# A graph layer woven into an MLP: the account that deals out its steps begins lower at a raised rate, with two more empty steps before the first weights

## The chip, the cores and the metric

One core of a Trainium2 chip runs the whole program in one launch. The metric is device microseconds (us) of one execution. TensorE (PE) does the matmuls, and its weight loads (PEld) overlap them. VectorE (DVE), ScalarE (ACT) and GpSimd (POOL) do the rest, and each engine works through its own queue in order. DMAs are issued from the queues of SP, ACT and POOL. TensorE's clock can be throttled, and the profile gives the clock that was granted as a share of full speed.

## The reference

The input is `x` with 1250 tokens of 768 features, and a graph of 21250 edges (`src`, `dst`, self loops among them, to which the graph layer adds another set). All is float32. With `xn = layernorm(x)`:

```python
# two graph attention layers; n = 1250
e = leaky_relu(s_src[src] + s_dst[dst], 0.2)
emax = segment_max(e, dst); ee = exp(e - emax[dst])
alpha = ee / segment_sum(ee, dst)[dst]
out = segment_sum(alpha * h[src], dst) + bias       # 4 heads of 192, then 2 heads of 96
gnn = concat([xn, out2]) @ Wu + bu
...
# linear attention with 12 heads, then an MLP 768 -> 3072 -> 768 with gelu
h = xn + linear_attention(layernorm(xn))
mix = h + gelu(layernorm(h) @ fc1_w + fc1_b) @ fc2_w + fc2_b
...
x = x + gnn + mix
x = x + two_of_four_experts(layernorm(x))           # 768 -> 1536 -> 768, routed by the pooled tokens
```

## The kernel before

Tokens lie in 10 tiles of 125. Both graph layers are computed densely: a table in DRAM holds for each pair (source, target) how many edges there are. It is made by 170 indirect DMAs from POOL's queue (L311), alternately into two tables, which are later added into one (`merged`, L1224), 125 rows at a time. POOL issues these merges behind the last of the indirect DMAs.

The stages, in order: features, keys, values and queries, the attention's output, the MLP of the mix, and the experts. The graph layers have no stage of their own. They are written as a generator, `gnn()`, and their steps are dealt out between the matmuls of the MLP of the mix:

- **The MLP.** 12 groups of 256 hidden units (`GROUPS`), each in two parts of the tokens (`MIX`, 2 x 250 and 2 x 375 columns). `fc1_unit` makes seven products of three matmuls each (a matmul in float32 is two instructions in the profile), with sums by Strassen's scheme, in the letters `P` of a pattern. Its evacuations are copies on ACT (L1152, L1162, L1165), sums on DVE (L1155, L1168, L1175) and Gelus on ACT (L1135). `fc2_half` (letter `h`) multiplies hidden units with half the columns of `fc2_w` for one tile of tokens (L1186, four instructions) and adds the sum to the result on DVE (L1191). Its PSUM tile is one of three banks, which `bank()` also hands to the transposes of the graph's steps. `load_fc1` (L898, 768 KB) and `load_fc2` (L905) load weights from SP's queue. DVE makes the sums of weights (L115 to L118).
- **The account.** `spend(us)` is called after each product (charged 2.04 or 1.36 us) and each half (1.39 us). It adds `rate * us` to a credit. While the credit covers the price of the last step, it pays it and takes the next step from `gnn()`, which yields its own price. So the account sets where in the program's text a graph step stands. A scheduler then orders the instructions of each engine; what is wrapped in `pin` keeps its order.
- **A search (`largest`)**, once for each graph layer: the largest source score for each target. It issues the first merges (first search only) and fetches of the table (`fetch`, L1237, POOL), yields a `lead` (17 us in the first search), and then goes through 10 pieces of 125 sources: one DVE instruction that masks the piece (L1252), and one for each head that takes the maximum (L1260 for the first piece, L1256 for the others), 10 us charged for a piece with four heads, 4.5 with two. Then come transposes (L1270) and reductions (L1274), a few small sums, a transpose of the result to one row (L1290), a copy (L1294), and the row's write to DRAM (`b_d`, L1295, from ACT's queue).
- **Weights and sums (`weighted`, `lagging`)**: for each head and each of three groups of target tiles, `bt` is read back from `b_d`, broadcast over the partitions (L1303, POOL). For each piece of sources: two exponentials on ACT (L1314, L1317), a maximum and a product with the table on DVE (L1319, L1320), and the matmuls that add up the weighted features (L1364 in the first layer, L1403 in the second), one piece behind the weights. A step is charged 1.7 us. The second layer ends with a projection (L1416) added to the result (L1423).

ACT needs another table for the exponentials than for the Gelus, so a switch between them is an `ACT_TABLE_LOAD`.

When the last group's second part begins, a loop takes all steps that are left at once. After that the tiles' LayerNorm and transposes (`last_tile`) run between the last halves.

Of the kernel before, what the change touches and what calls it, by code (L numbers as in the profile page):

```python
# [32 lines left out]
def tile_gps_layer(ctx, tc, a, out):  # L33
# [52 lines left out]
    def bank(name):  # L86
        return p_mm[0].tile([128, 512], F32, name=name, tag="mm")
# [556 lines left out]
    with tc.tile_pool(name="kvp", bufs=1) as kvp:  # L644
# [185 lines left out]
        for t in range(5):  # L830
            def before(t=t):
                if t == 1:
                    by_tokens(vec, xt, TP, TP)
                if t == 2:
                    by_tokens(vec, xt, 2 * TP, 3 * TP)
                    for vv in vvs:
                        pin(nc.vector.memset(vv[:, :, 128:129], 1.0))
# [379 lines left out]
    def rest(n):  # L1217
        for _ in range(n):
            yield 2.5
# [8 lines left out]
    def largest(heads, s, b_d, pace, before=lambda c: None, behind=lambda: None, lead=9.0):  # L1228


        run = slot_x[:TP, : heads * N].rearrange("p (h n) -> p h n", n=N)
        load = [slot_x[:TP, 5000 + i * N : 5000 + (i + 1) * N] for i in range(2)]
        load.append(turns[:TP, 0, :N])

        def fetch(c):
            if c < NT:
                pin(nc.gpsimd.dma_start(load[c % 3], adj_d[c * TP : (c + 1) * TP, :]))  # L1237

        for c in range(3):
            before(c)  # L1240
        fetch(0)
        fetch(1)
        yield lead
        for c in range(NT):
            before(c + 3)
            fetch(c + 2)
            if c == NT - 1:
                behind()
            adj = load[c % 3]

            far = turns[:TP, 1, :N]
            pin(nc.vector.tensor_scalar(far, adj, -2.0 * NEG, NEG, op0=ALU.mult, op1=ALU.add))  # L1252
            for h in range(heads):
                sc = s[:, 0, h, c : c + 1]
                if c:
                    pin(nc.vector.scalar_tensor_tensor(  # L1256
                        run[:, h, :], far, sc, run[:, h, :], op0=ALU.min, op1=ALU.max
                    ))
                else:
                    pin(nc.vector.tensor_scalar(run[:, h, :], far, sc, None, op0=ALU.min))  # L1260
                if h % 2:
                    yield pace
        yield from rest(2)
        mx = gp.tile([TP, heads, NT], F32, name=f"mx{heads}")
        for h in range(heads):
            for u0 in range(0, NT, 4):
                n = min(4, NT - u0)
                ps = bank("ps_mx").rearrange("p (u c) -> p u c", c=128)
                for u in range(n):
                    pin(nc.tensor.transpose(  # L1270
                        ps[:TP, u, :TP], run[:, h, (u0 + u) * TP : (u0 + u + 1) * TP],
                        ident[:TP, :TP],
                    ))
                nc.vector.tensor_reduce(  # L1274
                    mx[:, h, u0 : u0 + n], ps[:TP, :n, :TP], AX.X, ALU.max
                )
            yield 2.0
        sd = s[:, 1]
        b = gp.tile([TP, 2, heads, NT], F32, name=f"b{heads}")
        m = small.tile([TP, heads, NT], F32, name=f"m{heads}", bufs=1)  # L1280
        nc.vector.tensor_tensor(mx, mx, sd, ALU.add)
        nc.vector.scalar_tensor_tensor(m, mx, 0.2, mx, op0=ALU.mult, op1=ALU.max)
        nc.vector.tensor_tensor(b[:, 0], sd, m, ALU.subtract)
        nc.vector.scalar_tensor_tensor(
            b[:, 1], sd, 0.2, m, op0=ALU.mult, op1=ALU.subtract
        )
        yield from rest(2)
        n = 2 * heads * NT
        ps = bank("ps_row")
        pin(nc.tensor.transpose(  # L1290
            ps[:n, :TP], b.rearrange("p j h t -> p (j h t)"), ident[:TP, :TP]
        ))
        row = small.tile([80, TP], F32, name="row", bufs=1)
        nc.vector.tensor_copy(row[:n], ps[:n, :TP])  # L1294
        nc.scalar.dma_start(b_d, row[:n])  # L1295
        yield from rest(4)

    def weighted(g, h, heads, b_d, s, sl):

# [47 lines left out]
    def gnn():  # L1347
        feats = {}

        def fetch(h):  # L1350
            gh = turns[:TP, h % 2, :].rearrange("p (t f) -> p t f", f=193)
            pin(nc.gpsimd.dma_start(gh, rows(g1_d[h % 4], TP)))
            feats[h % 4] = gh

        yield from largest(4, s1, b1_d, 5.0, merged, lambda: fetch(0), 17.0)
        fetch(1)
        for g, (t0, n) in enumerate(SPLITS):
            for h in range(4):
# [15 lines left out]
                for i in range(n):  # L1374
# [9 lines left out]
                    if h == 3:  # L1384
                        for j in range(2):
# [5 lines left out]
                            nc.vector.tensor_reduce(s2[:, j, :, t0 + i], pr, AX.X, ALU.add)  # L1391
        nc.vector.tensor_scalar(s2l, s2[:, 0], 0.2, None, op0=ALU.mult)
        yield from largest(2, s2, b2_d, 4.5)
        load_wu2x()
        parts = earlier()
# [74 lines left out]


    steps = gnn()
    credit, cost = -44.0, 0.0

    def spend(us):
        nonlocal credit, cost
        credit += 1.06 * us
        while cost is not None and credit >= cost:
            credit -= cost
            cost = next(steps, None)  # L1480
# [15 lines left out]
    def put_half(g, c, t, j):  # L1496
        fc2_half(g, c, t, j)
        spend(1.39)
        if g == GROUPS - 1 and j:
            last_tile(t)  # L1500

    todo = []
    for g in range(GROUPS):
        if g:
            load_fc1(g + 1)
            load_fc2(g, 1)
            load_fc2(g + 1, 0)
        for c, pattern in enumerate(("PPhhhhPhhPPhhPPhhhh", "PPhhPhhPPhhPPhh")):
            if g == GROUPS - 1 and c:
                for _ in steps:  # L1510
                    pass
                cost = None
                gnn_pool.__exit__(None, None, None)
            parts = fc1_unit(g, c)
            if g == 0 and c:
                pattern = "PhPhhPhhhPhhPPP"
            for p in pattern:
                if p == "P":
                    next(parts)
                    if g or c:  # L1520
                        spend(2.04 if c else 1.36)
                elif todo:
                    put_half(*todo.pop(0))
            todo = halves_of(g, c)
# [197 lines left out]
    def second(i, t):  # L1722

        g = slots[i // 3]["g"][:TP]
        w11, w12, s3, w22, s1, s2, s4 = seconds[i]
        h11, t3, h21, h22 = quarters(i)

        def put(o, v):
            pin(nc.vector.scalar_tensor_tensor(o, v, g, o, op0=ALU.mult, op1=ALU.add))  # L1729

        ts = slice(t * TP, (t + 1) * TP)
        t1, t2, t4 = (ht[:, k, :, ts] for k in range(3))
        y1, y2 = y[:, t, :], y[:, t + NT // 2, :]
        p1, p5, p7 = (bank(n)[:TP, :384] for n in ("ps_r1", "ps_r5", "ps_r7"))
        p6 = bank4("ps_r6").rearrange("p a b -> p (a b)")[:TP, :384]
        c1 = u3 = mp.tile([128, 384], F32, name="c1")[:TP]
        u2 = mp.tile([TP, 384], F32, name="v2", bufs=2)
        product(mat, p1, h11[:, :, ts], w11)
        pin(nc.scalar.copy(c1, p1))
        product(mat, p6, t2, s2)  # L1740
        pin(nc.vector.tensor_tensor(u2, p6, c1, ALU.add))
        product(mat, p7, t3[:, :, ts], s3)
        pin(nc.vector.tensor_tensor(u3, p7, u2, ALU.add))
        product(mat, p5, t1, s1)
        put(y2[:, 384:], p5)
        put(y2[:, 384:], u3)
        yield
        product(mat, p1, h21[:, :, ts], w12, more=True)
        put(y1[:, :384], p1)
        product(mat, p7, t4, w22, more=True)  # L1750
        put(y1[:, 384:], p7)
        put(y1[:, 384:], u2)
        product(mat, p5, h22[:, :, ts], s4, more=True)
        put(y2[:, :384], p5)
        put(y2[:, :384], u2)
        yield
# [112 lines left out]
    rest, held, acts = [], [], []  # L1869
    for i in range(6):  # L1870
        for u in range(4):
# [31 lines left out]
            if i and u == 0:  # L1903
                if i > 1:
                    second_sums(i - 1)
                rest = [second(i - 1, t) for t in range(NT // 2)]
# [66 lines left out]
```

## Time and profile before

| | us |
|---|---|
| median of 3 runs (1900.64 to 1905.47) | 1905.28 |
| the profiled execution, its own time | 1904.38 |
| its span, first to last instruction | 1902.6 |
| PE busy, of the span | 1860.4 (98%) |
| DVE busy | 1326.4 (70%) |
| ACT busy | 811.1 (43%) |
| POOL busy | 502.7 (26%) |

An execution is divided into 40 slices of 47.6 us in the page's second part, with a digit for the busy tenths. A busy PE is not PE at its peak, since matmuls are pipelined and a matmul that waits in the pipeline counts as busy. A wait is listed with the engine and the line that ended it; where that one had long been done, it was another, often a DMA.

The last indirect DMA of the table is issued at 571.15, the first three merges at 575.44. The merges are issued on POOL in the order 0, 1, 2, then fetch 0, fetch 1, merge 3, fetch 2, and so on:

```
575.44  merges 0, 1, 2      586.70  fetch 0      593.76  fetch 1
594.29  merge 3             599.73  fetch 2      606.67  fetch 3
```

### The profile page before, as it was taken

The page shows a single profiled execution, that of the slowest core. Times are in us where ns is not written, and L with a number is a line of the kernel's source. Part 1 is how long each engine was busy: PE and PEld are TensorE (multiplying, and loading weights), DVE is VectorE, ACT ScalarE, POOL GpSimd, SP SyncE. Part 2 cuts the span into 40 slices and gives each one's busy share as a digit, 9 for nine tenths or more (in the row PEclk, how much of TensorE's full clock was granted, in tenths as well). Part 3 has the DMA queues.
Part 4 walks back from the last instruction along what each step waited for, and adds up shares of the span by engine and source line. Part 5 has one row for each costly group of instructions (what it writes and reads, how often), then busy time and mean ns, then how long its engine had stood idle before and what let it go on. Part 6 is the DMA issues. An engine that isn't in the chain of part 4 may idle for free.

```text
span 1902.6 us, 19523 instructions
## 1 busy us (share of the span) xinstructions
PE 1860.4 (98%) x6936; PEld 1235.7 (65%) x6936; DVE 1326.4 (70%) x2407; ACT 811.1 (43%) x1231; POOL 502.7 (26%) x341
## 2 busy tenths in 40 slices
PE   8999999999996999999999999999999999999998
PEld 7555556855564667787777655566766666666664
DVE  4656692668534976676766968766777777777778
ACT  3233321333410118777774176655373353433330
POOL 2275666786883120111210111100131000000000
PEclk9999999999998999999999999999999999999999
DMA  9748532526129842232443632201485202011023
GB/s 337 225 94 217 126 86 53 126 16 109 6 26 154 168 122 68 78 101 79 110 105 80 158 90 82 76 13 60 130 98 84 73 0 67 2 66 46 13 87 109
DMA packets 185934, 177.85 MB, mean 93 GB/s; under 512 B 110131, under 2 KB 155243, under 8 KB 184556
## 3 DMA queue, kind: packets, MB, share of 16 engines
q0 software_dynamic: 126640, 68.01, 20.9%
q1 hardware_dynamic: 55918, 100.83, 17.0%
q10 hardware_dynamic: 3278, 7.75, 1.3%
q8 instruction: 55, 0.90, 0.2%
q14 instruction: 43, 0.35, 0.1%
HBM read 140.11 MB, written 42.08 MB: 96 GB/s over the span
## 4 chain that ended last, share of the span: by engine, by line
PE 79%; DMA 7%; POOL 5%; issue 5%; DVE 2%; ACT 1%; ACTq 1%; SPq 0%; DVEq 0%; POOLq 0%
PE ps_f L1186 14%; PE ps_p L82 13%; PE ps_r L82 12%; PE ps_o L1364 7%; PE ps_a L128 7%; POOL tab L311 5%; DMA slot_a<-in_x_dram 3%; PE ps_c L128 3%; PE ps_g L574 3%; PE ps_f L1767 3%; PE ps_o L1403 2%; PE ps_va L128 2%; PE ps_ka L128 2%; PE ps_d L128 2%; PE ps_u L1416 1%
## 5 line engine op out<-in xcount | busy, mean ns | idle before, releaser
L311 POOL DMA_INDIRECT tab<-mult,place_e x170 | 355.7, 2092 | 163.3 <-DMA tab<-mult,place_e 118.1
L1186 PE MATMUL ps_f<-w,v 128*125 128x384 f32 x960 | 339.8, 489 | 15.1 <-DVE slot_a L1191 15.1
L1186 PEld LDWEIGHTS ps_f<-w,v 128*125 128x125 f32 x960 | 178.4, 189 | 122.5 <-DVE slot_a L1191 16.3
L1191 DVE TENSOR_TENSOR slot_a<-ps_f,slot_a 125x384 f32<-125x384 f32 x240 | 131.4, 553 | 71.6 <-PE ps_f L1186 67.8
L1319 DVE TENSOR_TENSOR wt<-ee 125x375 f32<-125x375 f32 (+1 forms) x180 | 106.0, 590 | 86.6 <-PE ps_o L1364 53.0
L1364 PEld LDWEIGHTS ps_o<-turns,wt 125*125 125x125 f32 x800 | 137.2, 188 | 28.4 <-DVE wt L1320 3.9
L1364 PE MATMUL ps_o<-turns,wt 125*125 125x193 f32 x800 | 151.1, 329 | 3.0 <-DVE wt L1320 3.0
L1314 ACT ACTIVATE ee<-bt,s 125x375 f32<-125x375 f32 (+1 forms) x180 | 114.8, 638 | 85.4 <-DVE wt L1319 70.9
L82 PE MATMUL ps_p<-fT,w 128*128 128x312 f32 (+1 forms) x432 | 125.5, 426 | 0.6 <-ACT c L1685 0.6
L1320 DVE SCALAR_TENSOR_TENSOR wt<-wt,slot_x 125x375 f32<-125x375 f32 (+1 forms) x180 | 105.7, 590 | 4.4
L82 PEld LDWEIGHTS ps_p<-fT,w 128*128 128x128 f32 x432 | 81.5, 189 | 36.2 <-ACT c L1685 1.1
L82 PE MATMUL ps_r<-w,slot_a 128*125 128x384 f32 x260 | 94.5, 486 | 0.0
L128 PE MATMUL ps_a<-fT,w 128*128 128x250 f32 (+1 forms) x288 | 85.0, 426 | 0.7 <-DVE slot_a L1031 0.7
L1729 DVE SCALAR_TENSOR_TENSOR slot_x<-ps_r,gate,slot_x 125x384 f32<-125x384 f32 x100 | 60.7, 615 | 33.3 <-PE ps_r L82 33.0
L82 PE MATMUL ps_p<-xt,ws 128*128 128x313 f32 (+1 forms) x288 | 83.6, 425 | 0.0
L1135 ACT ACTIVATE v<-v,par 128x250 f32<-128x250 f32 (+1 forms) x72 | 39.9, 555 | 98.0 <-DVE v L1168 42.4
L574 PE MATMUL ps_g<-fx,zT 128*125 128x388 f32 x240 | 80.1, 490 | 1.5 <-ACT zT L364 1.5
L541 PE MATMUL ps_u<-wu,fT 128*125 128x384 f32 x240 | 79.9, 487 | 0.5 <-ACT fT L527 0.4
L1256 DVE SCALAR_TENSOR_TENSOR slot_x<-turns,s,slot_x 125x1250 f32<-125x1250 f32 x54 | 79.4, 1512 | 0.0
L1317 ACT ACTIVATE ee<-bt,s1l 125x375 f32<-125x375 f32 (+1 forms) x120 | 75.4, 629 | 0.1
L82 PE MATMUL ps_r<-w2s,ht 128*125 128x384 f32 x200 | 72.7, 486 | 0.0
L128 PEld LDWEIGHTS ps_a<-fT,w 128*128 128x128 f32 x288 | 53.9, 189 | 25.6 <-issue 2.1
(427 smaller groups left out, 3422.6 us busy)
## 6 DMA issues: line engine op xcount, KB each, us to landing
turns<-g_d POOLq DMA_DIRECT2D x12, 942.4 KB
w<-in_L_mix_fc_w_dram SPq DMA_DIRECT2D x12, 768.0 KB
w<-in_L_mix_fc_w_dram SPq DMA_DIRECT2D x24, 384.0 KB
slot_x<-tab POOLq DMA_DIRECT2D x14, 610.4 KB
w<-in_L_ffn_w_dram SPq DMA_DIRECT2D x11, 768.0 KB
w<-in_L_ffn_w_dram SPq DMA_DIRECT2D x5, 1536.0 KB
slot_x<-tab POOLq DMA_DIRECT2D x40, 183.1 KB
kr_l<-key_d SPq DMA_DIRECT2D x6, 1062.5 KB
```

The costliest lines, as they stand in the source:

```text
L82: return lambda *args, **kw: pin(getattr(self.engine, name)(*args, **kw))
L128: engine.matmul(ps, wt[:, k, :], x[:, k, :], start=k == 0 and not more, stop=k == n - 1, skip_group_check=more,)
L311: nc.gpsimd.indirect_dma_start(out=tabs[c % 2][:, :], out_offset=bass.IndirectOffsetOnAxis(ap=place[:, c : c + 1], axis=0), in_=mult[:, c ...
L541: nc.tensor.matmul(ps[:TP, :w], fT[:, k, tc_], wu[:, k, c0 : c0 + w], start=k == 0, stop=k == KC - 1,)
L574: nc.tensor.matmul(ps[:TP, :388], zT[:, k, :], fx[:, k, h2 * 388 : (h2 + 1) * 388], start=k == 0, stop=k == KC - 1,)
L1186: nc.tensor.matmul(ps, v_of[c][:, f, h, at : at + TP], lasts[g, j][:, f, :], start=f == 0, stop=f == 1,)
L1191: nc.vector.tensor_tensor(o, ps, o, ALU.add)
L1256: pin(nc.vector.scalar_tensor_tensor(run[:, h, :], far, sc, run[:, h, :], op0=ALU.min, op1=ALU.max))
L1314: nc.scalar.activation(e[:, 0, :w], bt[:TP, 0, :w], AF.Exp, bias=s[:, 0, h, c : c + 1])
L1319: nc.vector.tensor_tensor(wt[:, :w], e[:, 0, :w], e[:, 1, :w], ALU.max)
L1320: nc.vector.scalar_tensor_tensor(wt[:, :w], wt[:, :w], 1.0, adj, op0=ALU.min, op1=ALU.mult)
L1364: nc.tensor.matmul(sums[i // 2][:TP, (i % 2) * 193 : (i % 2 + 1) * 193], wt[:, i * TP : (i + 1) * TP], gh[:, c, :], start=c == 0 and i % 2 ...
```

## The change

Three numbers are different. The account begins at -64 us in place of -44, so that the first graph step stands later between the MLP's matmuls. The rate is 1.09 in place of 1.06, so that the steps then follow each other more closely. And after the row's write, `largest` yields six empty steps of 2.5 us in place of four, before the first weights of that layer; as `largest` serves both layers, this is so in both. The instructions themselves are the same; only their order on the engines moves.

```diff
@@ largest
         row = small.tile([80, TP], F32, name="row", bufs=1)
         nc.vector.tensor_copy(row[:n], ps[:n, :TP])
         nc.scalar.dma_start(b_d, row[:n])
-        yield from rest(4)
+        yield from rest(6)
...
     steps = gnn()
-    credit, cost = -44.0, 0.0
+    credit, cost = -64.0, 0.0
 
     def spend(us):
         nonlocal credit, cost
-        credit += 1.06 * us
+        credit += 1.09 * us
         while cost is not None and credit >= cost:
             credit -= cost
             cost = next(steps, None)
```

## The prediction

> **What bounds the kernel now.** I read the busy time by slices first, then the waits of PE, then stretches of 20 us, then the order in time around each gap. PE is the bound: 98% busy. What can change is only the time in which it is not, or runs at half clock, while the account deals out steps (some 545 to 1340 us).
>
> ```profile
> PE   8999999999996999999999999999999999999998
> PEclk9999999999998999999999999999999999999999
> ```
>
> The one dip is near 600 us. The waits of PE and DVE in that stage name three gaps:
>
> ```profile
> PE ps_f L1186 <- DVE slot_a L1191: 15.1, 1, 15.1
> PE ps_o L1403 <- DVE wt L1320: 3.3, 1, 3.3
> PE ps_o L1364 <- DVE wt L1320: 3.0, 1, 3.0
> ...
> DVE turns L1252 <- DMA slot_x<-tab: 20.5, 1, 20.5
> ```
>
> Stretches (first PE, PEld, DVE, ACT, POOL busy, then granted clock, DMA share, GB/s): each gap is followed by a lower clock, and beside the gaps PE is full, even where DVE is.
>
> ```profile
> 580.00:600.00 20.00, 9.05 (x29) 5.06 (x27) 0.11 (x1) 0.94 (x2) 2.97 (x5) 0.80 1.30 147
> 600.00:620.00 20.00, 15.89 (x46) 9.99 (x47) 19.31 (x24) 2.45 (x5) 6.44 (x6) 0.77 1.20 205
> 620.00:640.00 20.00, 20.00 (x73) 13.39 (x72) 20.00 (x26) 2.77 (x7) 6.14 (x6) 1.00 1.24 204
> ...
> 720.00:740.00 20.00, 16.98 (x80) 14.49 (x79) 15.07 (x26) 19.11 (x29) 0.72 (x1) 0.91 0.02 8
> ...
> 1100.00:1120.00 20.00, 16.69 (x50) 9.41 (x49) 12.99 (x22) 13.87 (x22) 0.72 (x2) 0.91 0.26 71
> ```
>
> In time around the first gap: the scatter ends, the first merge takes 11 us, the first piece of the table is fetched at 586.70 and used at 600.65; DVE stands at that use (L1252) from 580.1, and every L1191 behind it holds a PSUM bank that PE needs.
>
> ```profile
> 586.70 0.57 POOL L1237 DMA_DIRECT2D slot_x<-tab  x1 [6.64 <-ACT c L1165]
> 600.65 1.16 DVE L1252 TENSOR_SCALAR turns<-slot_x 125x1250 f32<-125x1250 f32 x1 [20.55 <-DMA slot_x<-tab]
> 604.11 2.92 PE L1186 MATMUL ps_f<-w,v 128*125 128x384 f32 x4 [15.06 <-DVE slot_a L1191]
> ...
> 706.83 0.32 ACTq L1295 DMA_DIRECT2D b_d<-row  x1
> 717.30 0.71 ACT L1314 ACTIVATE ee<-bt,s 125x500 f32<-125x500 f32 x1 [4.85 <-DMA bt<-b_d]
> 723.77 4.44 PE L1364 MATMUL ps_o<-turns,wt 125*125 125x193 f32 x16 [3.02 <-DVE wt L1320]
> ```
>
> From the row's write (706.83) to the first exponential (717.30) are 10.5 us; the other two gaps are this latency, once per search. The price of half clock: in slices of 1 us the clock is 0.58, 0.50, 0.50, 0.71 from 725 to 729, so 1.7 us lost; the same by the slices after 1107; after the long gap 0.50 from 604.1 to 608 and 0.72 to 610, so 2.5. **Now lost: 15.06 + 2.5, 3.02 + 1.7, 3.31 + 1.7, together 27.3 us.** No change of the account alone can win more in this stage.
>
> **The change, part by part.** Nothing is added to or removed from the arithmetic. The account's us are not device us: a half is charged 1.39 and is four matmuls of 322 ns (1.29; 616.86 to 620.7 holds three), so one charged us is 0.93 device us.
>
> *Lower start and rate.* The first step needs 44/1.06 = 41.5 charged us now, 64/1.09 = 58.7 then; with the lead of 17 the first use of a piece goes from 57.5 to 74.3, 15.6 device us later. The data does not move with it: in the built programs' order POOL's queue is the same up to and through the searches' fetches, the first fetch waits for the first merge and otherwise for work long done, and the merge waits for the scatter. So I keep 600.65. In the built order DVE now has, ahead of L1252, five more L1191, L1168, L1175, L115 and L116. PE from 587.60 without a gap: two halves (2.58), two products of six 375-wide matmuls (1.89 each, 583.82 to 585.71), a half: 595.25; DVE evacuates it by 596.0 and waits 4.7 us there, not 20.5. PE goes on: a half, two products of 250 (1.27 each), two halves: 601.66, three banks full. The first bank comes free after L1252 (1.16) and one L1191 (0.55): 602.4, a gap of 0.7. The next bank's L1191 stands behind four L1260 (1.74 + 1.64), L117, L1155, L118 (1.3): 607.5 against 603.7, a gap of 3.8. **4.5 us, and 1.7 of half clock.**
>
> The fc1 load of 768 KB (L898, SP) is released by the matmuls that now end at 592, not at 610.05, so it falls into the fetch of the first piece. Bounds: 0 (it takes bytes from the later merges only) to 4.9 (768 KB at the 156 GB/s of 592 to 594 us, all before the fetch). By its queue's share (100.83 MB in 17.0% of the span) it is 2.5 us of all engines: I take **2.5**, since the DMA share is over 1 there. [...]
>
> *The rate in the searches.* A piece of the first search is 0.8 + 4 x 1.47 = 6.7 us of DVE against 10 charged us, 8.77 device us of cover before (10/1.06 x 0.93), 8.53 after: 0.24 less, ten times; in the second search 0.11, ten times: 3.5 us if PE pays it all, 0 if the banks absorb it. The rows lean to 0 (DVE full from 620 to 660, PE too): I take **1.0**. In the weighting steps DVE and ACT have 2 to 7 us of 20 free and PE's sum is the same: 0.
>
> *Two more empty steps.* They shift the first weights by 5/1.09 x 0.93 = 4.3 us, on paper more than 3.0 and 3.3. In the built order it is otherwise for the first search: between the row's transpose (L1290) and the first weighting matmul stand 14.3 us of PE work, 14.9 before; and ACT's queue now has the copy L1162 behind the first exponential, which waits for the 10.5 us. PE needs that copy after four halves, a product and two halves (9.0 us); it is there about 1.1 (row copied and issued) + 10.5 + 0.7 after the row: 12.3. **A gap of 3.3 and 1.7 of half clock remains**, on another wait. If ACT's order did not bite, it would be 0. In the second search the distance grows from 10.5 to 14.3; needed are 13.9 (1093.52 to 1107.40). But a table switch for two Gelus (L1135, 1.28 us each way) stands between the first and the second pair of exponentials: 0 to 2.1, I take **0.7**, too short to cost clock.
>
> *The end.* The steps cost 544 charged us, now 554 (four more rests of 2.5); dealt are 567.6: 567.6 x 1.06 - 44 = 557.7 before, 567.6 x 1.09 - 64 = 554.7 now. They still end before the loop that empties the rest (by 0.7, before by 13.7); the last tiles' LayerNorm comes two passes later, so 0. If one step were left it would be 1.5 charged us.
>
> [...]
>
> **Sum.** Left: 4.5 + 1.7 + 2.5 + 1.0 + 3.3 + 1.7 + 0.7 = 15.4. Gain 27.3 - 15.4 = 11.9. The profiled execution took 1904.4 (span 1902.6): 1892.5. The median of the runs, 1905.3, is 0.9 above it: **1893**.
>
> **Rivals.**
> - *All three gaps go*, as the arithmetic of the account alone says: only the 1.0 is left, 1904.4 - 26.3 = 1878. For it: 4.3 us of shift exceed both short gaps. Against: ACT's order, and the 600.65.
> - *The second gap goes too*, the first stays: 5.0 lower, 1888. It needs the row's trip under 7 us (10.5 now, b_d 4.7 and bt 5.2 in the chain of waits).
> - *The load costs its upper end and the next two pieces come late as well*: 4.9 instead of 2.5, and 3 us more in all at the second and third L1252, which follow at the pace of DVE with the pieces 6 to 7 us apart: 1898.
> - *Slower: the fetches move with the account.* The first fetch is dealt 18.6 charged us later (41.9 to 60.5), 17.3 device us. If POOL's issue moved by that, the piece would land at 618, the first gap be 4.5 + 17.3 with 2.5 of clock, and 1.0 + 3.3 + 1.7 + 0.7 come on top: 31.0 left, 3.7 more than now: 1908. For it: the row at 586.70 names ACT's L1165, 0.3 us before, as releaser. Against: fetches one, two and three are 7.1 and 6.0 us apart, the pace of merges, and ACT's copy has no part in the piece. It decides from a first fetch 13.6 us late (27.3 less the other 13.7), about 600.
> - *It doesn't do what it says*: the scheduler puts DVE's first use back where it was, no change. Against: the built order.
>
> **How the numbers follow.** Forecast 0.60, own range 1889 to 1897 (load 0 to 4.9, rate 0 to 3.5, second row 0 to 2.1); all gone 0.08; second gone 0.12; late pieces 0.12; slower 0.05; no change 0.03. About 0.3%, 5.7 us, is what a measurement can tell here: below 1899.6 is faster: 0.60 + 0.08 + 0.12 and 0.09 of the late pieces, 0.89; the rest of these, no change, and the part of the slower case under 0.3% make same 0.08; slower 0.03. The range takes in the second-gap case and the late pieces: 1886 to 1900.
>
> **What would show it.** First fetch within 2 us of 586.7, L1252 waiting 4 to 9 us instead of 20.5; PE gaps before L1186 of 3 to 8 us in sum near 600; a PE wait of 3 to 4 us for ACT's L1162 (at ps_a, L128) after the first L1290, in place of the wait at L1364; none over 2 us at L1403; PE full from 620 to 690. Wrong if the first fetch moves, if L1162 starts before the first L1314, or if new PE waits appear between 740 and 1080.

## The result, and the profile after

| | before | changed |
|---|---|---|
| median of 20 runs each, us | 1902.92 (1897.40 to 1911.11) | 1892.87 (1888.04 to 1900.67) |
| ratio, 95% interval | | 0.9949 (0.9936 to 0.9963) |
| profiled execution, its own time | 1904.38 | 1889.61 |
| its span | 1902.6 | 1887.8 |

The forecast of 1893 is met, and the change is faster by 10 us (7 to 12 by the interval). The profiled execution lies at the low end of its 20 runs, which will matter: another execution had a larger first gap.

The page of the changed kernel, in 40 slices: the dip of PE and of its clock is gone.

```profile
PE   8999999999999999999999999999999999999998
PEclk9999999999999999999999999999999999999999
```

The waits of PE (line waited at, engine and line that ended it, sum, times, longest): the long wait for a PSUM bank is gone, the copy on ACT is there as forecast, and L1403, in the weights of the second search, has four short waits.

```profile
PE ps_a L128 <- ACT u L1162: 3.7, 1, 3.7
PE ps_o L1403 <- DVE wt L1320: 3.1, 4, 1.1
...
PE ps_c L128 <- DVE ws L115: 0.7, 1, 0.7
```

The timeline (start, us, engine, idle time before it in brackets) around the first fetch and the first weights:

```profile
569.29 1.99 POOL L311 DMA_INDIRECT tab<-mult,place_e  x1 [0.30 <-issue]
...
585.16 0.57 POOL L1237 DMA_DIRECT2D slot_x<-tab  x1 [7.02 <-DVE slot_a L1191]
...
592.78 0.37 SPq L898 DMA_DIRECT2D w<-in_L_mix_fc_w_dram  x1
...
597.80 0.81 DVE L1252 TENSOR_SCALAR turns<-slot_x 125x1250 f32<-125x1250 f32 x1 [1.05 <-DMA slot_x<-tab]
604.08 1.53 PE L1186 MATMUL ps_f<-w,v 128*125 128x384 f32 x4 [0.46 <-DVE slot_a L1191]
...
702.61 0.32 ACTq L1295 DMA_DIRECT2D b_d<-row  x1
...
713.62 0.71 ACT L1314 ACTIVATE ee<-bt,s 125x500 f32<-125x500 f32 x1 [9.39 <-DMA bt<-b_d]
714.24 0.35 ACT L1162 COPY u<-ps_a 128x250 f32<-128x250 f32 x1
714.64 2.87 PE L128 MATMUL ps_a<-fT,w 128*128 128x250 f32 x6 [3.67 <-ACT u L1162]
```

DVE came to the first piece at 596.75 (597.80 less the wait of 1.05), where the forecast had 596.0. But the scatter's last L311 was issued at 569.29, not at 571.15, and the piece was there at 597.80 instead of about 603: the wait of DVE is 1 us, not 4 to 9, and PE's is half a us. The second gap is what the prediction says to a few tenths (its half clock is not: 2.6 us lost, 1.7 forecast): ACT's queue holds L1162 behind the exponential that waits 9.39 us for `bt`, and PE waits 3.67 us for that copy.

Stretches (PE, PEld, DVE, ACT, POOL busy, then granted clock, DMA share, GB/s): most of what is left lies in these three, and PE is full from 620 to 640 and from 660 to 700.

```profile
640.00:660.00 20.00, 19.26 (x70) 12.93 (x69) 20.00 (x26) 3.35 (x7) 1.07 (x2) 1.00 0.75 143
...
700.00:720.00 20.00, 16.33 (x53) 11.41 (x52) 7.57 (x15) 7.33 (x13) 3.06 (x5) 0.83 0.54 171
...
1100.00:1120.00 20.00, 18.21 (x51) 8.76 (x50) 15.38 (x27) 19.58 (x29) 0.20 (x1) 1.00 0.09 23
```

### The profile page after: what moved, and what is told of

It reads as the page before. It is cut to its first block, busy times and chain, and to the rows that moved or that the text cites. A ratio compares the mean times of both kernels' runs of the same rounds, so it can differ in the third digit from the quotient of the medians.

```text
span 1887.8 us, 19528 instructions
## 1 busy us (share of the span) xinstructions
PE 1858.4 (98%) x6936; PEld 1234.3 (65%) x6936; DVE 1329.0 (70%) x2407; ACT 808.0 (43%) x1229; POOL 498.4 (26%) x341
## 4 chain that ended last, share of the span: by engine, by line
PE 78%; issue 7%; DVE 5%; POOL 4%; DMA 4%; ACT 1%; ACTq 0%; SPq 0%; DVEq 0%; POOLq 0%
PE ps_p L82 13%; PE ps_r L82 12%; PE ps_f L1186 11%; PE ps_o L1364 7%; PE ps_a L128 5%; PE ps_u L541 4%; POOL tab L311 4%; PE ps_g L574 3%; PE ps_f L1767 3%; PE ps_c L128 3%; PE ps_va L128 2%; PE ps_ka L128 2%; PE ps_qa L128 2%; DVE slot_x L1256 2%; PE ps_o L1403 1%
## 5 line engine op out<-in xcount | busy, mean ns | idle before, releaser
L311 POOL DMA_INDIRECT tab<-mult,place_e x170 | 351.4, 2067 | 166.2 <-DMA tab<-mult,place_e 119.3
L1186 PE MATMUL ps_f<-w,v 128*125 128x384 f32 x960 | 337.0, 486 | 0.5 <-DVE slot_a L1191 0.5
L1186 PEld LDWEIGHTS ps_f<-w,v 128*125 128x125 f32 x960 | 177.5, 187 | 107.3 <-issue 8.3
L1191 DVE TENSOR_TENSOR slot_a<-ps_f,slot_a 125x384 f32<-125x384 f32 x240 | 131.6, 555 | 69.7 <-PE ps_f L1186 65.9
L1364 PEld LDWEIGHTS ps_o<-turns,wt 125*125 125x125 f32 x800 | 136.1, 187 | 25.1 <-issue 0.5
L1364 PE MATMUL ps_o<-turns,wt 125*125 125x193 f32 x800 | 149.3, 327 | 0.0
## 6 DMA issues: line engine op xcount, KB each, us to landing
turns<-g_d POOLq DMA_DIRECT2D x12, 942.4 KB, 13.7
```

Source lines behind the costliest of these rows:

```text
L311: nc.gpsimd.indirect_dma_start(out=tabs[c % 2][:, :], out_offset=bass.IndirectOffsetOnAxis(ap=place[:, c : c + 1], axis=0), in_=mult[:, c ...
L1186: nc.tensor.matmul(ps, v_of[c][:, f, h, at : at + TP], lasts[g, j][:, f, :], start=f == 0, stop=f == 1,)
L1191: nc.vector.tensor_tensor(o, ps, o, ALU.add)
L1364: nc.tensor.matmul(sums[i // 2][:TP, (i % 2) * 193 : (i % 2 + 1) * 193], wt[:, i * TP : (i + 1) * TP], gh[:, c, :], start=c == 0 and i % 2 ...
```

## The experiments

Twelve kernels, in three groups of four, each group on another chip; each was timed beside its own runs of the kernel before, with medians of 1905.78, 1903.84 and 1905.99. Ratios are against those, so kernels of different groups are compared by ratio and not by median. Three things were to be told apart: which of the three numbers (start, rate, empty steps) carries the gain; whether the first piece of the table has a time of its own; and what the fc1 load beside its fetch costs.

### The start and the rate without the empty steps

```diff
-    credit, cost = -44.0, 0.0
+    credit, cost = -64.0, 0.0
...
-        credit += 1.06 * us
+        credit += 1.09 * us
```

> Start -64 and rate 1.09 of the change, but four empty steps before the first weights as before. My theory (the gain is the first gap; the two more empty steps are worth nothing): PE's wait near 604 under 1 us as in the changed kernel's profile, the wait of 3 to 4 us for ACT's copy L1162 is there as well, the second search's L1403 waits 0.5 to 2 us in sum; ratio to the kernel before 0.992 to 0.996. Rival (the empty steps carry part of the gain, gaps two and three come back at 3 us each with their half clock): PE waits of 3 us or more at L1364 or L1403, ratio 0.997 to 0.999.

Ratio 0.9934 (0.9913 to 0.9955), median 1891.92. The wait for L1162 is there with 3.7 us. L1403 waits 0.2 us, less than the 0.5 to 2 that I had expected, and the first gap is 1.8 us, more than the 1 us. The two empty steps are not needed for the gain: without them the time is not longer, and the third gap is smaller than with them.

### The empty steps alone

```diff
-        yield from rest(4)
+        yield from rest(6)
```

> Only the two more empty steps; start -44 and rate 1.06 as before. My theory: the first gap stays at 13 to 16 us (PE L1186 waiting for L1191, near 600), the wait for the first weights of the first search is about 3 us as before, since the row's trip out and back (10.5 us) and the order of ACT set it, the second search's L1403 waits 1 to 3 us; ratio 0.998 to 1.001. Rival (4.3 us of shift close both short gaps): waits at L1364 and L1403 under 0.5 us, ratio 0.994 to 0.996.

Ratio 0.9977 (0.9962 to 0.9992), median 1901.53. PE's waits of this kernel:

```profile
PE ps_f L1186 <- DVE slot_a L1191: 14.7, 1, 14.7
PE ps_o L1364 <- DVE wt L1320: 3.0, 1, 3.0
```

The first two gaps are as before, as expected. But no wait at L1403 is listed at all, where I had expected 1 to 3 us: in this execution the third gap, 3.3 us and 1.7 of half clock, is gone, and the medians say much the same (4 us). The longer distance is one part of it. The other is that the row's trip took 7.9 us here (1098.40 to 1106.27), not 10.5: the first weights were ready 13.6 us after the row's transpose, with 14.2 us of PE work to cover them, and with a trip of 10.5 they would have come some 2 us late. So the third gap is 0 with the steps alone, 0.2 with the start and the rate alone, and 1.7 with all three, and the parts of the change do not add up there.

### Half the start

```diff
-    credit, cost = -64.0, 0.0
+    credit, cost = -54.0, 0.0
```

(against the changed kernel)

> Start -54 in place of -64, all else as in the change. My theory (the piece of the table lands at its own time, 597 to 601, whatever the account does, and DVE's use of it stands at 585): DVE L1252 waits 12 to 15 us, PE loses 7 to 10 us near 595 plus half clock, first fetch still issued at 585 to 587; ratio 0.997 to 0.999. Rival (fetches move with the account): first fetch about 8 us earlier than in the changed kernel, first gap as in the changed kernel, ratio 0.994 to 0.996.

Ratio 0.9995 (0.9981 to 1.0010), median 1905.31: none of the gain, and both theories missed. The timeline:

```profile
591.60 0.57 POOL L1237 DMA_DIRECT2D slot_x<-tab  x1 [7.00 <-issue]
591.86 0.37 SPq L898 DMA_DIRECT2D w<-in_L_mix_fc_w_dram  x1
...
610.06 0.81 DVE L1252 TENSOR_SCALAR turns<-slot_x 125x1250 f32<-125x1250 f32 x1 [25.90 <-DMA slot_x<-tab]
613.46 4.12 PE L128 MATMUL ps_c<-fT,ws 128*128 128x375 f32 x6 [21.64 <-DVE v L1168]
```

The profiled execution is the slowest of the twelve runs (1909.35), so its gap is not that of the median. The gap is 21.6 us, larger than the 15.1 of before. Two things came together: the scatter ended 4.2 us later than in the profile before (its last L311 at 575.38), and the load was issued 0.26 us behind the fetch, which then took 18.5 us. The fetch does not follow the account either: it is later here than with the start at -64, where the rival has it 8 us earlier.

### A later start

```diff
-    credit, cost = -64.0, 0.0
+    credit, cost = -74.0, 0.0
...
-        credit += 1.09 * us
+        credit += 1.11 * us
```

(against the changed kernel)

> Start -74 and rate 1.11, six empty steps. DVE's first use of a piece comes at about 603, after the piece in every execution. Theory A (what is left of the changed kernel's loss in slow executions is its first gap, which varies with when the piece lands): no DVE wait at L1252, no PE wait near 604, and the median 2 to 4 us below the changed kernel's: ratio 0.991 to 0.994, and its runs lie closer together. Theory B (the first gap is already gone in nearly every execution of the changed kernel, and its spread has another source): same first stage, ratio as the changed kernel, 0.994 to 0.996, spread the same 12 us; the PE wait for first weights stays about 3 us in both.

Ratio 0.9913 (0.9892 to 0.9933), median 1889.11, six runs from 1885.97 to 1891.80. DVE comes to the piece at 602.4 and waits 1.02 us, PE has no wait near 604. The first weights cost 3.0 at L1364 and the second search 2.8 at L1403. These are theory A's numbers, but for the 1 us that DVE still waits; with six runs against twenty the narrower spread is a hint only.

### The changed kernel once more

> The changed kernel as it is, once more. My theory (its first gap is set by a race: DVE stands at the first use of a piece at 596.7, the piece lands some 28 us after the scatter's last instruction, which comes at 569 to 575 in different executions, and later when the fc1 load at 592 falls into the fetch; the first profile caught an early scatter): if the last L311 is at 571 or later, DVE L1252 waits 4 to 8 us and PE loses 3 to 7 us near 604; if it is at 569, under 1.5 us. Median ratio to the kernel before 0.994 to 0.996. Rival (the first gap is always as small as in the first profile): PE under 1 us near 604 whatever the scatter's end, first piece at 597 to 598.

Ratio 0.9967 (0.9951 to 0.9983), median 1898.54, twelve runs from 1890.45 to 1902.27: above the 0.994 to 0.996 that I had expected, with an interval that overlaps the first. The profiled execution took 1893.27, span 1891.5.

```profile
567.83 1.99 POOL L311 DMA_INDIRECT tab<-mult,place_e  x1 [0.30 <-issue]
...
584.27 0.57 POOL L1237 DMA_DIRECT2D slot_x<-tab  x1 [7.62 <-DVE slot_a L1191]
...
598.92 0.81 DVE L1252 TENSOR_SCALAR turns<-slot_x 125x1250 f32<-125x1250 f32 x1 [3.66 <-DMA slot_x<-tab]
605.20 2.89 PE L1186 MATMUL ps_f<-w,v 128*125 128x384 f32 x4 [3.07 <-DVE slot_a L1191]
```

The rival falls: in this execution of the same kernel the first gap is 3.07 us, and the slices of 1 us behind it show the clock at 0.50 for six us and 0.93 in the seventh, 3.1 us lost. My own rule was half wrong: the scatter ended still earlier (567.83), and DVE waited 3.66 us all the same, since the piece took 14.65 us. The scatter's end is not the only thing that varies.

### The load moved away from the fetch

```diff
+        if c == 7: pin(load_fc1(3, nc.gpsimd.dma_start))
...
-            load_fc1(g + 1)
+            if g != 2: load_fc1(g + 1)
```

(against the changed kernel; the first line stands in `merged`, and `load_fc1` takes the queue as an argument)

> The changed kernel with one load moved: the 768 KB fc1 load of the third group (L898, SP, at 592) is issued from POOL's queue behind the merge of the eighth piece, some 30 us later; all of PE's, DVE's and ACT's order is that of the changed kernel. Theory A (the load costs the first piece 2 to 5 us in executions with a late scatter): the piece lands 12 to 14 us after its fetch is issued whatever the scatter's end, and the median is 1.5 to 3 us below the changed kernel's: ratio 0.9925 to 0.9943. Theory B (the load takes its bytes from merges that nothing waits for): ratio as the changed kernel, 0.9943 to 0.996.

Ratio 0.9957 (0.9941 to 0.9972), median 1895.01, timed beside the same runs of before as the run above. The piece took 14.3 us. In this execution the scatter ended at 573.79, so DVE waited 6.44 us, and PE 2.20 and 2.66 us with a clock of 0.50 in the slices from 605.5 to 614.5. The time lies in theory B's range, and its interval overlaps that of the changed kernel: by the time alone the load's cost can't be told from nothing here.

### The load moved, with half the start

> Start -54, rate 1.09, six empty steps, as in the run with the half start, and the same load moved away from the first fetch. Theory A (with the half start the load was issued in the moment of the first fetch and made it 18.4 us long in place of 13): the fetch lands 12 to 14 us after issue, PE's gap near 593 is 9 to 13 us in place of 21.6, ratio 0.9965 to 0.9985. Theory B (the half start loses because DVE stands at the piece with L1168 behind it, which PE needs sooner than a bank, and a late scatter; the load has no part): gap 15 us or more, ratio 0.999 to 1.001 as without the move.

```profile
585.75 0.57 POOL L1237 DMA_DIRECT2D slot_x<-tab  x1 [6.28 <-PE ps_a L128]
...
599.69 1.12 DVE L1252 TENSOR_SCALAR turns<-slot_x 125x1250 f32<-125x1250 f32 x1 [15.69 <-DMA slot_x<-tab]
603.10 4.12 PE L128 MATMUL ps_c<-fT,ws 128*128 128x375 f32 x6 [11.44 <-DVE v L1168]
```

Ratio 0.9980 (0.9965 to 0.9996), median 1899.55. The fetch took 13.9 us in place of 18.5, PE's gap was 11.4 us in place of 21.6: theory A's numbers. The 11.4 that is left is what theory B names: DVE stands at the piece, and L1168 behind it. Of the 10.2 us between the two gaps, 4.8 are the earlier scatter (its last L311 at 570.57, not 575.38) and 4.5 the shorter fetch (13.94, not 18.46). The run with the load in place was in another group, on another chip, and the two intervals overlap.

### The first fetch held back

```diff
+        for i in range(6 if heads == 4 else 0): pin(nc.gpsimd.memset(turns[:TP, 1, :N], 0.0))
```

(in `largest`, ahead of the first merges; against the changed kernel. The second of the two runs has the load moved as well.)

> The changed kernel with six MEMSETs of 128x1250 on POOL (1.1 us each by the one that the profile has) between the scatter's last instruction and the first merge: some 2 us of them lie in POOL's wait for the scatter, so the first fetch comes about 4.6 us later, at 588 to 593; nothing else moves. It forces what I think a late scatter does by itself. My theory: the fetch meets the fc1 load of 592, takes 15 us or more, the piece lands at 605 to 609, DVE waits 8 to 12 us, PE loses 6 to 10 us and half clock behind it near 604; the time is 5 to 10 us above the changed kernel's: ratio 0.998 to 1.002. Rival (a late piece is absorbed, and the changed kernel's spread has another source): ratio as the changed kernel, 0.994 to 0.997.

> The same six MEMSETs, and the load moved behind the eighth merge. Theory A (the load beside the fetch costs it 2 to 5 us): the fetch issued at 588 to 593 lands 13 to 14.5 us later, at 602 to 606, DVE waits 5 to 9 us, and the time is 2 to 5 us below the run with the load in place: ratio 0.995 to 0.999. Theory B (the load costs nothing): ratio as the run with the load in place, within 1 us.

The six MEMSETs took 7.9 us, not 6.6, and the scatter ended late in both executions (575.77 and 577.91), so the fetches came at 596.69 and 597.81. With the load in place the piece took 16.65 us, DVE waited 17.1 and PE 12.9 and 2.0; ratio 0.9986 (0.9968 to 1.0003). With the load moved it took 13.96 us, DVE waited 13.5 and PE 9.2 and 2.0; ratio 0.9979 (0.9962 to 0.9996).

```profile
613.34 0.81 DVE L1252 TENSOR_SCALAR turns<-slot_x 125x1250 f32<-125x1250 f32 x1 [17.14 <-DMA slot_x<-tab]
...
614.67 2.92 PE L1186 MATMUL ps_f<-w,v 128*125 128x384 f32 x4 [12.90 <-DVE slot_a L1191]
```

These rows, of the run with the load in place, show the chain from a late fetch to the end: the gain of the change is gone, within the interval, when the first piece comes some 15 us later. The load costs 2.7 us in the fetch; in the medians, 1905.61 and 1904.40, it is not separated from nothing.

### All that was learnt, put together

```diff
-        yield from rest(6)
+        yield from rest(8)
...
-    credit, cost = -64.0, 0.0
+    credit, cost = -72.0, 0.0
...
-        credit += 1.09 * us
+        credit += 1.13 * us
```

(against the changed kernel, with the load moved; the second run has the load in place, the third a start of -76 and the load moved)

> Start -72, rate 1.13, eight empty steps before the first weights of each search, and the load moved. If each gap is what the account and the row's trip make it, none is left over 2.5 us: DVE reaches L1252 at 598, L1162 stands ahead of the first L1314 in both searches, eight steps cover the row's trip of 10.5 us; PE waits in the stage 3 to 6 us in sum against 8 in the changed kernel's first profile; ratio 0.988 to 0.991 (1880 to 1886). Rival (the denser steps, 1.13 in place of 1.09, cost PE what the gaps give back): new PE waits behind DVE or ACT between 620 and 700 or 1110 and 1160 of 3 us and more, ratio 0.993 to 0.996.

> Start -72, rate 1.13, eight empty steps, with the load left where it is (SP, about 592): tells what the moved load is worth in the fastest run. DVE reaches L1252 at 598. With the load the piece lands at 598 to 604 by the scatter's end, so DVE waits 0 to 6 us and PE 0 to 4 in some executions: theory A 0.5 to 2.5 us above the run with the load moved, ratio 0.990 to 0.993. Theory B (the load costs nothing): 0.9895 to 0.991, same as the run with the load moved.

> Start -76 in place of -72, rate 1.13, eight empty steps, load moved. DVE reaches L1252 at 603, after the piece in nearly every execution: no wait there. If the first gap still costs the run with -72 something in executions with a late scatter, this one is 0.5 to 2 us faster: ratio 0.989 to 0.9905. Rival (by then the first gap is gone, and the 1.4 charged us that are left at the end and the closer steps cost as much): the same, 0.990 to 0.992.

| start, load | median (runs) | ratio, interval | PE's waits in the stage over 0.5 us |
|---|---|---|---|
| -72, moved | 1883.04 (4) | 0.9905 (0.9884 to 0.9926) | 1.7 at L1165, 0.6 at L1270 |
| -72, in place | 1887.69 (6) | 0.9885 (0.9853 to 0.9918) | 6.0 at L1186, 1.2 at L1165, 0.6 at L1270 |
| -76, moved | 1883.23 (6) | 0.9880 (0.9850 to 0.9909) | 2.0 at L1186 (721), 0.9 at L1270 |

All three beat both kernels, by 18 to 23 us against before; they can't be ranked by these intervals, and the last two gained more than any of their theories had said. No denser step cost PE anything that shows: the rate of 1.13 was no new bound. In the run with the load in place the scatter ended at 573.55, the load came 3.6 us behind the fetch (592.38 and 588.79), and the piece was used at 605.77, after DVE had waited 8.03 us for it.

How the second gap closed, in the run with -72 and the load moved: the copy now stands ahead of the exponential and its table load, and PE's next wait is the next copy, 1.7 us long.

```profile
703.43 0.32 ACTq L1295 DMA_DIRECT2D b_d<-row  x1
707.89 0.37 ACT L1162 COPY u<-ps_a 128x250 f32<-128x250 f32 x1 [5.51 <-PE ps_a L128]
708.28 1.28 ACT L1314 ACT_TABLE_LOAD   x1
715.07 0.71 ACT L1314 ACTIVATE ee<-bt,s 125x500 f32<-125x500 f32 x1 [5.51 <-DMA bt<-b_d]
...
717.29 1.53 PE L128 MATMUL ps_a<-room,w 128*128 128x250 f32 x6 [1.74 <-ACT c L1165]
```

The trip of the first search's row, from L1295 to the first exponential, is 11.6 us here, 11.0 in the changed kernel, 10.5 before: it did not get shorter; what stands behind it in ACT's queue did change. These runs change start, rate and empty steps together; none puts the copy ahead alone.

## Why the prediction came out as it did

**The account moves PE's steps, not the data: right.** The fetch followed the scatter in every kernel. In the twelve profiles without MEMSETs it was issued 15.0 to 16.8 us behind the last L311, whatever the start (-44 to -76). The rival in which the fetches move with the account is out.

**"So I keep 600.65": the step that failed.** One execution's time was taken for the kernel's. All fourteen profiles, sorted by the time from fetch to load (DVE waited for the piece in all of them, so the use is the landing):

| kernel | last L311 | first fetch | load after fetch | fetch to use |
|---|---|---|---|---|
| before | 571.15 | 586.70 | 23.4 | 13.95 |
| empty steps alone | 571.09 | 587.86 | 21.5 | 12.5 |
| load moved: four kernels | 570.57 to 573.79 | 585.75 to 588.83 | over 35 | 13.5 to 14.3 |
| fetch held back, load moved | 577.91 | 597.81 | not near | 13.96 |
| changed, first profile | 569.29 | 585.16 | 7.6 | 12.6 |
| start and rate | 568.74 | 585.04 | 7.2 | 13.6 |
| changed, second profile | 567.83 | 584.27 | 7.0 | 14.65 |
| start -74 | 571.10 | 587.72 | 4.5 | 15.7 |
| start -72, load in place | 573.55 | 588.79 | 3.6 | 17.0 |
| half the start | 575.38 | 591.60 | 0.3 | 18.5 |
| fetch held back | 575.77 | 596.69 | -4.5 | 16.65 |

The scatter's last instruction comes between 567.8 and 577.9, though nothing ahead of it was edited. It is not a matter of the chip alone: within each group of four, on one chip, it spreads over 5.4 to 6.6 us. The chain of 2.3 us steps on POOL starts at 57.0 to 59.2 in all fourteen, and all have two or three long waits between 440 and 470, of 10.7 to 12.7 us in sum. The larger part of the spread is there before: the many waits ahead of 440, most of them for the chain's own DMAs, come to 92 to 99 us. Why they differ was not followed.

In the run with the load moved the piece did come at the forecast time: it was used at 603.14, where 600.65 and 2.5 make 603.15. DVE waited 6.4 us there, within the 4 to 9 of the forecast, and PE 4.9 us in two waits, where 4.5 and 2.5 were forecast: the chain from the piece to the banks is right, but the 2.5 us of a later piece are not all paid by PE.

**The load: the right bounds, and a race in place of a mean.** The prediction took 2.5 us between 0 and 4.9. Seven fetches with no load near took 13.7 us in the mean (12.5 to 14.3); with the load 7 us behind, 13.6; at 3.6 to 4.5, 15.7 and 17.0; at 0.3, 18.5. So the cost is 0 to 4.8 us, and which it is depends on two times that have nothing to do with each other: PE's progress, which releases the load at 591 to 593, and the scatter's end, which the fetch follows by 15.0 to 16.8 us. A late scatter is punished twice. The highest cost, 4.8 us, is nearly the load's own time (4.9 by the prediction's estimate, from 768 KB at 156 GB/s); how the two transfers share the engines was not shown.

**The other terms**, in us of PE, in the two profiled executions of the changed kernel:

| term | predicted left | first profile | second profile |
|---|---|---|---|
| first gap, with the load's 2.5 | 7.0 | 0.5 | 3.1 |
| half clock behind it | 1.7 | 0 | 3.1 |
| rate in the searches (`ws` L115, 640 to 660) | 1.0 | 0.7 | 0.7 |
| second gap (L1162) | 3.3 | 3.7 | 3.8 |
| half clock behind it | 1.7 | 2.6 | 2.5 |
| third gap (L1403, the first two waits) | 0.7 | 1.7 | 1.5 |
| weighting steps (L1403, the other two) | 0 | 1.3 | 1.2 |
| sum | 15.4 | 10.5 | 15.9 |
| gain against 27.3 | 11.9 | 16.8 | 11.4 |
| gain by the spans | | 14.8 | 11.1 |

The second profile has the predicted sum, to half a us, but not by the predicted terms: the first gap with its clock is 2.5 smaller, the second 1.3 and the third 0.8 larger, and the weighting steps, put at 0, cost 1.2.

The third term failed in "needed are 13.9". PE's work after the row's transpose (1087.10 in the first profile) lasted 14.35 us, as forecast; but the first weights came after 15.44, so PE waited 1.09 us there, ahead of any table switch.

```profile
1087.12 1.34 DVE L1205 MEMSET turns<- 1x1538 f32 x1 [0.38 <-issue]
...
1088.97 0.27 DVE L1294 COPY row<-ps_row 40x125 f32<-40x125 f32 x1
...
1091.16 1.44 POOL L1303 DMA_DIRECT2D bt<-b_d  x2 [0.91 <-DMA b_d<-row]
1091.25 0.37 SPq L905 DMA_DIRECT2D w<-in_L_mix_fc_w_dram  x1
```

The new order puts a MEMSET and an L1191 on DVE between the transpose and the row's copy, so the row is written 2.17 us behind the transpose (0.62 before). The trip from there is 10.3 us, nearly the 10.5 of before, but not by the same parts: the write is back sooner (1.9 us from L1295 to the issue of the read, 5.1 before), and the read of `bt`, from its issue to the first exponential, takes 8.4 us in place of 5.4. In the second search of all fourteen profiles this read takes 8.0 to 8.4 us where a 384 KB load (L905) is issued 0.1 us behind it, 6.9 to 7.0 where the load is 3.0 to 3.2 us behind, and 5.3 to 6.0 where none is issued in the 4.8 us behind it. It looks like the same race as at the first piece; no run moves this load, so that it is the cause is not shown.

The switch that the prediction names is there, two table loads of 1.28 us and the Gelus from 1100.88 to 1104.33, and the wait behind it is 0.64 us, inside its 0 to 2.1. The other two waits at L1403, 1.04 us at 1192.78 and 0.30 at 1233.91, lie in later weighting steps, where the prediction said "0"; before the change PE had no wait at L1403 there. All four (0.30 to 1.09 us) cost no clock, as said: it was granted at 1.00 in every stretch from 1100 to 1240. In the first profile 2 us of the terms' gain are not in the span: 0.9 of them are idle time of PE ahead of 545 us, where the change has no part (9.6 us, before 8.7); the rest was not followed.

**The other rivals.** "All three gaps go" did not come, and neither did "the second gap goes too": the copy behind the exponential held in all six profiles with the start at -64 (3.7 to 4.2 us); with -44, -54 and -74 PE waited at L1364 instead, 3.0 to 3.9 us; only with eight empty steps and the start at -72 or -76 is neither wait there. "The load at its upper end" is what a late scatter makes of the kernel, but in part of the executions.

**The agreement of the medians is in part luck.** The forecast's gain was 12 us from a base of 1905.3. Measured were 10 us (7 to 12) from a base of 1902.9, and 6 us (3 to 9) when the kernel was run once more. The mean gain is smaller than forecast. That the spread of the changed kernel, 1888 to 1902, is that of its first gap fits all profiles and the forced late fetch, but it is not shown: the changed kernel has only two profiles, both of faster executions, and the kernel before spreads as widely (1897 to 1911). The upper end of the forecast's own range does not follow from the three bounds named for it: together they give 1899, not 1897.

## What to carry to other kernels

When work is moved later to meet data, ask whether the data has one time or a spread, and what else the move sets in motion: here the same shift that hid a late piece also freed PE to release a 768 KB load into that piece's fetch (15.7 us with the start at -74 and the load 4.5 us behind, 13.7 in the mean with no load near). Half of such a shift gave nothing while the load stood beside the fetch (ratio 0.9995), and more of it gave more (0.9913); leave room for the late end of the spread. And an engine that works in order makes a wait for a DMA into a wait for all that stands behind it, as ACT's 9.39 us for `bt` became 3.67 us of PE for the copy behind: before adding empty steps, look at what lies behind the waiting instruction: the second gap was gone only where the copy came ahead of it and eight empty steps covered the trip; with the copy ahead and four or six steps (before, start -74) PE still waited 3.0 us for the weights.

## What the runs showed of the hardware

The granted clock does not go by the length of a gap alone. These are two slices of 1 us (columns as in the stretches above). First the run with -76, the second us behind a gap of 1.96 us that ended at 721.43:

```profile
722.43:723.43 1.00, 1.00 (x3) 0.45 (x2) 0.00 (x0) 0.99 (x2) 0.00 (x0) 0.50 0.06 16
```

Then the changed kernel with the load moved, the first us behind a gap of 3.86 us that ended at 723.12; all slices from 700 to 740 have a clock of 1.00:

```profile
723.12:724.12 1.00, 1.00 (x5) 0.91 (x6) 0.41 (x1) 1.00 (x2) 0.00 (x0) 1.00 0.82 309
```

The shorter gap halved the clock, the longer did not. Gaps of 2.6, 3.0, 3.1, 3.7 and 3.8 us halved it elsewhere, while one of 3.03 us (start -74) did not; what was lost behind a single gap, where it fell, was 1.5 to 3.1 us. Taken from where the clock falls, which can be inside the gap, the loss was 1.7 us (725 to 729 before the change, for one) or, to the digits of the slices, a whole multiple of it wherever they cover it whole: 3.4 after 713 in the changed kernel, 5.1 with the load moved, 6.8 with that and half the start, 8.5 at the first gap before the change, 11.8 with half the start alone. So the clock stood at half for 3.4 us or for a multiple of that. What decides whether a gap halves it was not shown: one of 1.96 us was enough, and one of 3.86 us was not.

The same chain of indirect DMAs, in kernels that are alike up to there, ended anywhere within 10 us (567.8 to 577.9, fourteen profiles).
